# Side work of VectorE in a fused attention and expert kernel, handed out by the room of each step

## The chip, the cores and the metric

The kernel runs on one core of one Trainium2 chip. The metric is device time in microseconds (us) of one execution; three runs of the kernel before are shown. Engines are named as in the profile: PE is TensorE's matmul and PEld its weight load, DVE is VectorE, ACT is ScalarE, POOL is GpSimd, SP is SyncE, which here only issues transfers.

## The reference

The input is a tensor of 2 batches, 256 channels and 56 x 56 places (3136 tokens per batch). Layer 0 is a non-local block without a softmax, with normalisation, residual and relu. Layer 1 is causal attention with 4 heads of 64, and then a mixture of 8 experts of which each token takes 2. Cut to what matters here:

```python
t = _to_tokens(x)                                   # 2 x 3136 x 256
t = t + _L1_attn_ref(_ln_t(t), W_attn, W_proj)      # q, k, v; softmax(q k / 8, causal) v; W_proj
t = t + _L1_ffn_ref(_ln_t(t), gate_w, gate_b, W1, b1, W2, b2)
# ffn: probs = softmax(xf @ gate_w); the two best experts per token;
#      out += prob[e] * (gelu(xf @ W1[e] + b1[e]) @ W2[e] + b2[e])
```

## The kernel before, in words

All data is f32. Layer 0 comes first and ends at about 90 us. Then come the attention of both batches (about 90 to 845 us), and the experts (845 us to the end). Within the attention, the order of every engine's instructions is the order in which the Python code issues them; nothing reorders it.

**Steps.** Queries are cut into 7 blocks of 448 columns (`W`, index `i`), heads into 2 pairs (`hp`), and keys into chunks of 128 (`j`). One step is one chunk of keys against one block of queries for one pair of heads. A step has two halves: `scores(n)` (matmuls on L804, the exponential on ScalarE on L808, for a chunk on the diagonal a mask on VectorE on L811, and VectorE's running sum of the exponentials on L822 or L827), and `values(n)` (matmuls on L855). The values run `LAG` = 3 steps behind the scores. Masked chunks, called cut, and whole chunks alternate at the end of each block; a cut chunk has fewer columns to do. In the last step of a block and pair, ScalarE copies the values out of their bank (L862), and GpSimd adds the two halves into `qT` (L863). The pool of the values' bank (`py`) has one buffer, that of the scores (`psc`) two, that of the exponentials (`st`) five.

**Visits.** Two steps behind the end of each block and pair (`BEHIND`, with the lag), the loop makes a visit: `visit` issues the matmuls of the projections ahead (queries and keys L613, values L628, transposes L599), and `products` those of the output projection (L682), with one add each on VectorE (L687). Behind it `sum_rows` sums the exponentials over the keys with matmuls of ones (L876), copies the result on ScalarE (L881) and stores it with four transfers on SP, and reads it back with a fifth.

**Later.** A list `later`, kept by a step counter `clock`, holds what follows on the sums: `invert` (a reciprocal of 7 columns on VectorE, L896, and three transfers) 4 steps on, `scale` (VectorE multiplies `qT` by the inverses, L908) 6 steps on, and `hand_on` 2 steps on, which allows the output projection of that block.

**Side work.** Generators in a queue hold the rest: statistics of finished rows (`closer`, L177 and L178, two instructions per chunk of 128 tokens), the choice of experts (`choose`, `dispatch`: some hundred small VectorE instructions per batch), scatters of the rows to their experts' slots (L1493 on VectorE, L1501 on GpSimd, two scatters per chunk), and loads of the experts' first weights on SP. One call of `pull` issues one piece. `between` is called once per step, ahead of its scores, and pulls one piece in every step, except in cut steps of block 0:

```python
tick[0] += 1
if not cut or i:
    pull()
```

In the last block of the last batch `between` also issues loads of the experts' second weights (`load_w2`). In the experts' stage `meanwhile` pulls what is left.

Of the kernel before, what the change touches and what calls it, by code (L numbers as in the profile page):

```python
# [28 lines left out]
def conv_attn_moe_kernel(  # L29
# [52 lines left out]
    P = 128  # L82
    B, C, N = x.shape
    NH = C // P
# [8 lines left out]
    W = 448  # L93
    NB = N // W
# [54 lines left out]
    def room(name):  # L149

        return tok.tile([P, NH * E * H], F32, tag="room", name=name)
# [18 lines left out]
    sum_d = nc.dram_tensor("sums", (NSUM, 2, W), F32, kind="Internal").ap()  # L170
# [340 lines left out]
    def layer1(nm, general):  # L511

        with ExitStack() as whole:
# [182 lines left out]
                    yield False  # L696

            unclosed = [NCH] * B

            def closer(b, first, m, k):  # L700

                for n in range(first, first + m):
                    stats(b, n, 1, k, bg, f"o{nm}{b}")
                    unclosed[b] -= 1
                    yield True

            def attend(qT, kT, v, fst, fs, psc, py, open_batch, visit, between, clock, later, finished):
# [156 lines left out]
                        del yps[b, hp, i]  # L864

                def sum_rows(b, hp, i):
                    yh = qT[:, hp, i * W : (i + 1) * W]
                    r = (b * NH + hp) * NB + i
                    sn = f"{nm}{b}_{hp}_{i}"
                    acc = accs[b, hp, i]  # L870
                    summed.add((b, hp, i))
                    sp = bank(f"sp_{b}_{hp}_{i}")

                    flat = acc.rearrange("p a w -> p (a w)")
                    for g in range(4):
                        nc.tensor.matmul(  # L876
                            sp[g * 32 : (g + 1) * 32, : W // 2], ones[:, :32],
                            flat[:, g * W // 2 : (g + 1) * W // 2], start=True, stop=True,
                        )
                    line = fs.tile([P, W], F32, tag="rb", bufs=3, name=f"line_{sn}")  # L880
                    nc.scalar.copy(line[:, : W // 2], sp[:, : W // 2])  # L881
                    halves = sum_d[r].rearrange("a (h w) -> (a h) w", h=2)
                    for g in range(4):
                        nc.sync.dma_start(
                            out=halves[g : g + 1], in_=line[g * 32 : g * 32 + 1, : W // 2]
                        )
                    nc.sync.dma_start(
                        out=sums[:, r], in_=sum_d[r].rearrange("a (p f) -> (a p) f", p=HS)
                    )
                    later.append((clock[0] + 4, invert, b, hp, i, yh))  # L890

                def invert(b, hp, i, yh):
                    r = (b * NH + hp) * NB + i
                    sn = f"{nm}{b}_{hp}_{i}"
                    back = fs.tile([P, 2 * W // P], F32, tag="back", name=f"back_{sn}")
                    nc.vector.reciprocal(back, sums[:, r])  # L896
                    nc.sync.dma_start(
                        out=inv_d[r].rearrange("a (p f) -> (a p) f", p=HS), in_=back
                    )
                    rb = fs.tile([P, W], F32, tag="rb", bufs=3, name=f"rb_{sn}")  # L900
                    for a in range(2):
                        nc.sync.dma_start(
                            out=rb[a * HS : (a + 1) * HS], in_=inv_d[r, a].partition_broadcast(HS)
                        )
                    later.append((clock[0] + 6, partial(scale, rb), b, hp, i, yh))

                def scale(rb, b, hp, i, yh):
                    nc.vector.tensor_tensor(yh, yh, rb, ALU.mult)  # L908
                    later.append((clock[0] + 2, hand_on, b, hp, i, yh))

                def hand_on(b, hp, i, yh):
# [2 lines left out]
                def due(now):  # L914
                    while later and (now is None or later[0][0] <= now):
                        _, task, b, hp, i, yh = later.pop(0)
                        task(b, hp, i, yh)
                        later.sort(key=lambda e: e[0])

                ends = {s[:2]: n for n, s in enumerate(steps)}  # L920
                LAG, BEHIND, FREED = 3, 2, 4
                visits = {BEHIND: (0, -1, NH - 1)}
# [4 lines left out]
                final = visits.pop(len(steps) + BEHIND)  # L927
                visits[len(steps) + 1] = final
                for n in range(len(steps) + LAG):
                    if n in visits:  # L930
                        visit(*visits[n])
                        b, i, hp = visits[n]
                        if i >= 0 and visits[n] != final:
                            sum_rows(b, hp, i)
                        aligned()
                    if n + 1 < len(steps) and n > LAG and steps[n][2] == 0 and steps[n - LAG - 1][2] == 0 and steps[n - LAG - 1][4]:
                        turn_rows(*steps[n][:2])
                    if n < len(steps):
                        b, i = steps[n][:2]
                        if n == 0 or steps[n - 1][0] != b:  # L940
                            open_batch(b)
                        between(b, i, ends[b, i] - n, (steps[n][3] + 1) * P > i * W + 1)

                    late = n >= LAG and steps[n - LAG][4]
                    if n >= LAG:
                        due(clock[0])
                        clock[0] += 1
                    if n >= LAG and not late:
                        values(n - LAG)
                    if n < len(steps):  # L950
                        scores(n)
                    if late:
                        values(n - LAG)
                sum_rows(final[0], final[2], final[1])
                return due

            def attend_general(b, qT, kT, v):
# [1128 lines left out]
            else:  # L2086
# [54 lines left out]
                def visit(b, i, hp):  # L2141

                    now, then = ahead(b, i, hp)
                    last = b + 1 == B and i + 1 == NB
                    if last and hp == 0:
                        assert ranked[0]
                        early_ids.extend(experts_of(0))
                    if last and hp + 1 == NH:
                        nc.scalar.activation(warm, eps5[:1], AF.Gelu)
                        while len(early_rows) < 2:  # L2150
                            pull(every=True)
                        now = [partial(early_input, n, qT) for n in range(2)]
                    ring.append(0)
                    for piece in now:
                        piece()
                    for _ in range(2):
                        products()
                    for piece in then:
                        piece()
                    ring.clear()  # L2160

                def between(b, i, left, cut):
                    if b == B - 1 and i == NB - 1 and left < NH * NCH - 2:

                        now = load_w2(left < NCH - 4)
                        for _ in range(1 if left > NCH - 4 else 2):
                            next(now, None)

                    tick[0] += 1
                    if not cut or i:  # L2170
                        pull()

                due = attend(
# [259 lines left out]
```

## Time and profile before

| | us |
|---|---|
| median of three runs | 1254.82 |
| lowest and highest | 1254.31, 1254.89 |
| profiled execution, its own time | 1272.23 |
| span of its instructions | 1270.5 |
| PE busy | 1247.3 |
| DVE busy | 773.9 |
| ACT busy | 613.1 |
| POOL busy | 356.2 |
| running sums L827, DVE | 344.5 in 344 instructions |
| exponentials L808, ACT | 330.7 in 400 instructions |

The span runs from the first to the last instruction of the one profiled execution. The mean granted clock of TensorE in it is 0.995. Busy times are sums over the span; PE's overlap its weight loads, and its ends are modelled. A line such as L827 is a line of the kernel before.

### The profile page before, as it was taken

Reading aid. Unit: us, or ns where it says so; the run is one execution under the profiler, and the core shown is the slowest. Engines: PE = TensorE matmul, PEld = TensorE weight load, DVE = VectorE, ACT = ScalarE, POOL = GpSimd, SP = SyncE. Lnnn points to the kernel's source line nnn. Section 1 sums busy time; section 2 is a strip of 40 time slices with the busy share of each in tenths; the row PEclk is TensorE's granted clock in tenths of the full one; section 3 lists DMA queues with packets and bytes.
Section 4 is the critical chain, followed back from the end, with each engine's and each line's share of the span. In section 5 each row is a group of like instructions: output and inputs, shape, how many; then the busy total and the mean of one; then the engine's idle time right before and its main releaser. Section 6 shows DMA issues by size and latency. Waiting matters only on the chain.

```text
span 1270.5 us, 28742 instructions
## 1 busy us (share of the span) xinstructions
PE 1247.3 (98%) x10881; PEld 857.1 (67%) x10881; DVE 773.9 (61%) x1687; ACT 613.1 (48%) x1237; POOL 356.2 (28%) x318
## 2 busy tenths in 40 slices
PE   8999999999999999999999999999999999999998
PEld 8876655555454645655555543469888999899996
DVE  2683567566766575576677887785743433455664
ACT  0255555565656565455555655563332333344442
POOL 1103231110021104211112766100266112666651
PEclk9999999999999999999999999999999999999999
DMA  9995101000000000100000223641344343466654
GB/s 314 354 345 187 25 23 37 25 15 26 14 17 16 7 20 17 36 21 14 9 16 25 71 67 110 202 136 61 101 135 151 101 114 101 142 200 200 212 164 125
DMA packets 118723, 125.66 MB, mean 99 GB/s; under 512 B 27223, under 2 KB 108488, under 8 KB 118578
## 3 DMA queue, kind: packets, MB, share of 16 engines
q1 hardware_dynamic: 107922, 97.19, 25.3%
q0 software_dynamic: 9840, 25.67, 6.0%
q8 instruction: 90, 1.47, 0.5%
q10 hardware_dynamic: 816, 0.88, 0.2%
q14 instruction: 55, 0.45, 0.1%
HBM read 62.06 MB, written 61.05 MB: 97 GB/s over the span
## 4 chain that ended last, share of the span: by engine, by line
PE 91%; DVE 4%; DMA 1%; issue 1%; ACT 1%; SPq 0%; DVEq 0%; ACTq 0%
PE sc_f L804 19%; PE yp_f L855 18%; PE ht_f L1637 14%; PE yp_f L1656 14%; PE qk_f L613 7%; PE v_f L628 4%; PE pp_f L682 3%; PE cp L410 3%; PE gram L317 2%; DVE acc_f L827 2%; PE tp_f L1614 2%; PE sp_f L876 1%; PE xp_f L599 1%; PE yo_f L1883 1%; DMA w1s_f<-in_w_dram 0%
## 5 line engine op out<-in xcount | busy, mean ns | idle before, releaser
L808 ACT ACTIVATE st_f<-sc_f 128x896 f32<-128x896 f32 (+5 forms) x400 | 330.7, 838 | 198.0 <-PE sc_f L804 178.9
L827 DVE TENSOR_TENSOR acc_f<-acc_f,st_f 128x896 f32<-128x896 f32 (+6 forms) x344 | 344.5, 1002 | 118.9 <-ACT st_f L808 109.1
L804 PE MATMUL sc_f<-qT_f,kT_f 64*64 64x448 f32 (+5 forms) x3136 | 347.5, 499 | 0.3 <-ACT st_f L808 0.3
L855 PE MATMUL yp_f<-st_f,v_f 64*64 64x448 f32 (+5 forms) x2928 | 328.0, 510 | 4.1 <-ACT acc_f L862 2.5
L804 PEld LDWEIGHTS sc_f<-qT_f,kT_f 64*64 64x64 f32 x3136 | 144.8, 133 | 128.9 <-issue 106.2
L1646 ACT ACTIVATE g_f<-ht_f,b1b 128x128 f32<-128x128 f32 x408 | 116.6, 371 | 227.3 <-PE ht_f L1637 123.4
L855 PEld LDWEIGHTS yp_f<-st_f,v_f 64*64 64x64 f32 x2928 | 125.1, 133 | 132.2 <-issue 99.3
L1637 PE MATMUL ht_f<-xT_f,w_f 128*128 128x128 f32 x1600 | 196.9, 276 | 5.2 <-issue 5.2
L1637 PEld LDWEIGHTS ht_f<-xT_f,w_f 128*128 128x128 f32 x1600 | 193.8, 192 | 9.1 <-issue 4.6
L1501 POOL DMA_INDIRECT x_slots<-xr_f,idx x100 | 120.4, 1204 | 147.0 <-DVE xr_f L1499 77.6
L863 POOL TENSOR_TENSOR qT_f<-acc_f 128x448 f32<-128x448 f32 x26 | 29.6, 1140 | 406.3 <-ACT acc_f L862 406.3
L1625 DVE COPY w_f<-w1s_f 128x1024 f32 x102 | 72.7, 713 | 90.0 <-PE ht_f L1637 34.2
L584 POOL TENSOR_SCALAR xn_f<-t 128x256 f32<-128x256 f32 (+1 forms) x50 | 82.4, 1655 | 129.4 <-DVE t L185 43.6
L1677 POOL DMA_INDIRECT y_tokens<-ys_f,to_f x57 | 59.2, 1038 | 125.2 <-DVE ys_f L1666 102.9
L613 PE MATMUL qk_f<-px_f,wat 128*128 128x512 f32 (+2 forms) x224 | 88.2, 546 | 0.6 <-ACT px_f L605 0.6
L1666 DVE TENSOR_TENSOR ys_f<-yp_f,kT_f 128x128 f32<-128x128 f32 x102 | 29.5, 289 | 92.3 <-PE yp_f L1656 69.5
L613 PEld LDWEIGHTS qk_f<-px_f,wat 128*128 128x128 f32 x224 | 40.6, 190 | 46.3 <-issue 41.7
L1656 PE MATMUL yp_f<-px_f,g_f 128*128 x204 | 62.3, 387 | 1.6 <-issue 1.6
L1656 PE MATMUL yp_f<-kT_f,g_f 128*128 x204 | 62.1, 386 | 0.0
L1656 PE MATMUL yp_f<-v_f,g_f 128*128 x204 | 61.8, 385 | 0.0
L1656 PE MATMUL yp_f<-w2s_f,g_f 128*128 x204 | 61.6, 384 | 0.0
L1834 POOL DMA_INDIRECT y_f<-y_slots,idx x50 | 55.5, 1110 | 17.1 <-issue 17.1
(299 smaller groups left out, 1302.4 us busy)
## 6 DMA issues: line engine op xcount, KB each, us to landing
x_slots<-fill SPq DMA_DIRECT2D x1, 8190.0 KB
xb_f<-x_slots SPq DMA_DIRECT2D x60, 130.0 KB
x_slots<-fill SPq DMA_DIRECT2D x1, 7296.0 KB
y_slots<-ys_f SPq DMA_DIRECT2D x57, 128.0 KB
kept<-t SPq DMA_DIRECT2D x2, 3200.0 KB
x<-in_x_dram SPq DMA_DIRECT2D x14, 448.0 KB
rb_f<-inverses SPq DMA_DIRECT2D x56, 112.0 KB
y_f<-y_tokens SPq DMA_DIRECT2D x23, 256.0 KB
```

The costliest lines, as they stand in the source:

```text
L584: nc.gpsimd.tensor_scalar(xn[:k, a], ts[b][:k, n + a, :C], ts[b][:k, n + a, MEAN : MEAN + 1], ts[b][:k, n + a, RSTD : RSTD + 1], ALU.subtr ...
L613: nc.tensor.matmul(ps[:, :w], wat[:, c, d0 : d0 + P], px[:, s % 2, c, :w], start=(c == 0), stop=(c == NH - 1),)
L804: nc.tensor.matmul(to, left, right, start=True, stop=True)
L808: nc.scalar.activation(st[rows, :, c0:], ps[rows, :, c0:W], AF.Exp, scale=SCALE)
L827: nc.vector.tensor_tensor(acc[rows, :, c0:], acc[rows, :, c0:], st[rows, :, c0:], ALU.add)
L855: nc.tensor.matmul(to, left, right, start=first, stop=end)
L1501: s = nc.gpsimd.indirect_dma_start(out=xds[b], out_offset=bass.IndirectOffsetOnAxis(ap=idxs[b][:kk, k, n : n + 1], axis=0), in_=xr[:kk], i ...
L1625: nc.vector.tensor_copy(w, w1s[:, :, bass.ds(e, 1), :].rearrange("p c e h -> p c (e h)"))
L1637: nc.tensor.matmul(ht[:, k, :], w[:, c, k * P : (k + 1) * P], xT[:, c, :], start=(c == 0), stop=(c == NH - 1),)
L1646: nc.scalar.activation(g[:, k, :], ht[:, k, :], AF.Gelu, bias=b1bs[b][:, k, i : i + 1])
L1656: nc.tensor.matmul(yp[:, :C], g[:, k, :], w2s[k][:, bass.ds(e, 1), :].rearrange("p e d -> p (e d)"), start=(k == 0), stop=(k == KH - 1),)
L1677: s = nc.gpsimd.indirect_dma_start(out=y_tokens, out_offset=bass.IndirectOffsetOnAxis(ap=to[:, n % GB : n % GB + 1], axis=0), in_=ys, in_o ...
```

## The change

It does four things.

1. A balance `spare`, in us, decides on side work. `room(n)` gives what a step leaves to VectorE: 1.5 us for a full block of columns, less 0.42 for a mask, less 0.07 + 1.02 for the running sum, scaled by the width. `between` adds it (to a balance of at most 1.0) and pulls a piece when the balance is above -0.8 (-0.9 while scatters of the first batch go on), which costs 0.35 (0.3). Statistics take another 0.25, a scaling 0.6.
2. A visit adds 2.0 to the balance (at most 2.0 in all), and at its end pulls pieces at 0.5 each (0.8 while sending) until the balance is 0.3 or less.
3. `sum_rows` issues the matmuls alone and returns the rest, `store_sums`, which is called behind the values of that step (when those are not a block's first). As the clock has been advanced by then, what follows on the sums is due one step later than before.
4. The scaling of the last block of the last batch is due 9 steps behind its inverses, the others 6.

The number of instructions on each compute engine and the work in them are the same.

```diff
             unclosed = [NCH] * B
+            spare = [0.0]
...
                 for n in range(first, first + m):
                     stats(b, n, 1, k, bg, f"o{nm}{b}")
+                    spare[0] -= 0.25
                     unclosed[b] -= 1
                     yield True
...
                 def sum_rows(b, hp, i):
...
                             flat[:, g * W // 2 : (g + 1) * W // 2], start=True, stop=True,
                         )
+                    return partial(store_sums, b, hp, i, sp)
+
+                def store_sums(b, hp, i, sp):
+                    yh = qT[:, hp, i * W : (i + 1) * W]
+                    r = (b * NH + hp) * NB + i
+                    sn = f"{nm}{b}_{hp}_{i}"
                     line = fs.tile([P, W], F32, tag="rb", bufs=3, name=f"line_{sn}")
                     nc.scalar.copy(line[:, : W // 2], sp[:, : W // 2])
...
-                    later.append((clock[0] + 6, partial(scale, rb), b, hp, i, yh))
+                    loading = b == B - 1 and i == NB - 1
+                    later.append((clock[0] + (9 if loading else 6), partial(scale, rb), b, hp, i, yh))

                 def scale(rb, b, hp, i, yh):
                     nc.vector.tensor_tensor(yh, yh, rb, ALU.mult)
+                    spare[0] -= 0.6
                     later.append((clock[0] + 2, hand_on, b, hp, i, yh))
...
+                def room(n):
+
+                    _, i, _, j, first, _, _ = steps[n]
+                    off = j * P - i * W
+                    width = W - max(0, off)
+                    return (
+                        2 * 0.75 * width / W
+                        - (0.42 if off > -P else 0)
+                        - (0 if first else 0.07 + 1.02 * width / W)
+                    )
...
                 for n in range(len(steps) + LAG):
+                    copy_sums = None
                     if n in visits:
                         visit(*visits[n])
                         b, i, hp = visits[n]
                         if i >= 0 and visits[n] != final:
-                            sum_rows(b, hp, i)
+                            copy_sums = sum_rows(b, hp, i)
                         aligned()
...
-                        between(b, i, ends[b, i] - n, (steps[n][3] + 1) * P > i * W + 1)
+                        between(b, i, ends[b, i] - n, (steps[n][3] + 1) * P > i * W + 1, room(n))

                     late = n >= LAG and steps[n - LAG][4]
                     if n >= LAG:
                         due(clock[0])
                         clock[0] += 1
                     if n >= LAG and not late:
                         values(n - LAG)
+                    if copy_sums:
+                        copy_sums()
                     if n < len(steps):
                         scores(n)
                     if late:
                         values(n - LAG)
-                sum_rows(final[0], final[2], final[1])
+                sum_rows(final[0], final[2], final[1])()
                 return due
...
                 def visit(b, i, hp):
...
                     for piece in then:
                         piece()
                     ring.clear()
-
-                def between(b, i, left, cut):
+                    spare[0] = min(spare[0] + 2.0, 2.0)
+                    while spare[0] > 0.3:
+                        spare[0] -= 0.8 if placed[0] and not sent[0] else 0.5
+                        pull()
+
+                def between(b, i, left, cut, room):
...
                     tick[0] += 1
-                    if not cut or i:
+                    spare[0] = min(spare[0], 1.0) + room
+                    sending = placed[0] and not sent[0]
+                    if spare[0] > (-0.9 if sending else -0.8):
+                        spare[0] -= 0.3 if sending else 0.35
                         pull()
```

More of the change, by code (lines that the diff above doesn't have):

```diff
@@ L866, in sum_rows @@
                 def sum_rows(b, hp, i):
-                    yh = qT[:, hp, i * W : (i + 1) * W]
-                    r = (b * NH + hp) * NB + i
-                    sn = f"{nm}{b}_{hp}_{i}"
                     acc = accs[b, hp, i]
@@ L879, in sum_rows @@
                         )
+                    return partial(store_sums, b, hp, i, sp)
[3 more added lines that the diff above has]
+                    sn = f"{nm}{b}_{hp}_{i}"
                     line = fs.tile([P, W], F32, tag="rb", bufs=3, name=f"line_{sn}")
                     nc.scalar.copy(line[:, : W // 2], sp[:, : W // 2])
-                    halves = sum_d[r].rearrange("a (h w) -> (a h) w", h=2)
+                    split = sum_d[r].rearrange("a (h w) -> (a h) w", h=2)
                     for g in range(4):
                         nc.sync.dma_start(
-                            out=halves[g : g + 1], in_=line[g * 32 : g * 32 + 1, : W // 2]
+                            out=split[g : g + 1], in_=line[g * 32 : g * 32 + 1, : W // 2]
                         )
```

## The prediction

> **What bounds the kernel now.** I read the page's busy shares and chain first, then the waits of TensorE, then the timeline at each of those waits. The busy line and the chain say that TensorE sets the time almost everywhere:
>
> ```profile
> PE 1247.3 (98%) x10881; PEld 857.1 (67%) x10881; DVE 773.9 (61%) x1687; ACT 613.1 (48%) x1237; POOL 356.2 (28%) x318
> ...
> PE 91%; DVE 4%; DMA 1%; issue 1%; ACT 1%; SPq 0%; DVEq 0%; ACTq 0%
> ```
>
> The first line is busy us per engine, the second the shares of the chain that ended last. So work taken from VectorE or ScalarE is worth nothing as such; only moments count in which TensorE waits for them. The waits of TensorE list these (us in total, times, longest):
>
> ```profile
> PE yp_f L855 <- ACT acc_f L862: 2.5, 4, 0.7
> PE yp_f L855 <- DVE st_f L811: 1.4, 3, 0.8
> ```
>
> The second row is what the change aims at: values held by VectorE's mask (L811). The longest stands in the timeline, in the second batch, four steps behind a projection:
>
> ```profile
> 519.28 1.32 DVE L827 TENSOR_TENSOR acc_f<-acc_f,st_f 128x896 f32<-128x896 f32 x1 [2.16 <-ACT st_f L808]
> ...
> 520.52 0.41 DVE L177 BATCH_NORM_STATS2 st_of<-t 128x6 f32<-128x256 f32 x1
> ...
> 523.38 1.24 PE L804 MATMUL sc_f<-qT_f,kT_f 64*64 64x448 f32 x8
> 523.90 0.42 DVE L177 BATCH_NORM_STATS2 st_of<-t 128x6 f32<-128x256 f32 x1
> 524.35 0.18 DVE L178 BATCH_NORM_AGGREGATE t<-st_of 128x2 f32<-128x6 f32 x1
> 524.45 0.61 DVE L908 TENSOR_TENSOR qT_f<-qT_f,rb_f 128x448 f32<-128x448 f32 x1
> ...
> 524.97 0.42 DVE L811 TENSOR_TENSOR st_f<-st_f,keep 128x256 f32<-128x256 f32 x1
> 525.42 0.69 DVE L827 TENSOR_TENSOR acc_f<-acc_f,st_f 128x512 f32<-128x512 f32 x1
> 525.45 0.66 PE L855 MATMUL yp_f<-st_f,v_f 64*64 64x192 f32 x8 [0.82 <-DVE st_f L811]
> ```
>
> Columns: start, us, engine. See that VectorE stood idle 2.16 us just before 519.28, and that the same engine then had three statistics pairs and a scaling handed to it within the narrow masked steps, so the mask came late. Scores start at 523.38 and the values behind them at 525.45: 2.07 us, where a full step in steady state takes 0.75 from scores to values (303.15 to 303.90 in the timeline). The loss is 1.32 us, more than the 0.82 shown as idle, as the pipe had to drain.
>
> **What the Trainium skill says.** "Perfetto Trace Analysis", Per-instruction lifecycle: a matmul's end is modelled, so starts are safer than ends; that is why I measure from start to start, and the 1.32 against 0.82 agrees. "TensorE: Matmul & The Clock Gate", Architectural detail: ScalarE and VectorE take their queues strictly in order. The lines above agree: the ready mask waits behind a scaling nobody is waiting for. "VectorE: DVE Perf Modes", Specifications and Mode 1x: 0.96 GHz, one f32 result a cycle for two tensors, so 896 take 0.93 us by estimate; the trace has 1.09, which I use. "GPSIMD Engine Reference", Specifications: GpSimd shares VectorE's SBUF ports when an instruction has two SBUF inputs; the add at 519.28 took 1.32 beside two GpSimd normalisations, against 1.09 alone, so crowding side work into projections is not free.
>
> **The change part by part.** No instruction is added or removed; the order moves.
>
> *Side work by room.* A full, unmasked step leaves 1.5 - 1.09 = 0.41 us by the new function's own constants, and a pull costs 0.35, so full steps go on pulling; masked steps leave nothing or less and skip. A visit (the place of the projections) gives 2.0 of credit, so up to four pulls follow it, three when sending or when statistics charge their 0.25. In the changed order, statistics that stood one per step on three or four steps behind a projection stand together behind the projection's adds. Worked out at the stall above: 2 pairs of 0.42 + 0.18 and one scaling of 0.61 move into the 2.16 us idle, 1.81 in all, so it fits; what is left in the four steps is the later scaling, one step further on, and the last pair, two further on. I take 1.3 us back. In the first batch the same place (scores 150.30, values 151.29) lost 0.99 - 0.75 = 0.24. The other masked steps where TensorE took longer than for the same step in the other batch or head pair, start of scores to start of scores: 166.46 (1.08 against 0.81), 169.04 (0.66 against 0.52), 654.64 (1.02 against 0.52), 723.72 (0.73 against 0.60), 758.56 (0.88 against 0.60). With the 0.24 these are 1.5; statistics or a scaling stand ahead of the mask in each, and the new order shifts most by one step to a full one. I take 1.0. The rank products, now inside a visit, leave step 624.95 but need a bank there: 0.
>
> *Scaling one step later.* The clock is read after it is advanced, so invert, scale and hand-on run a step later in all blocks. In blocks 1 to 4 this moves the scaling (0.61) from a masked to a full step (counted above), in block 5 from a full to a masked one, four times: unseen before, bounded by 0 and 4 x 0.3; I take +0.2 in all, as VectorE shows 0.4 us idle per full step there.
>
> *Sums' copy behind the values.* ScalarE's copy of the sums (0.345) now stands behind its copy of the values (0.91) and ahead of the exponential:
>
> ```profile
> 517.12 0.34 ACT L881 COPY line_f<-sp_f 128x224 f32<-128x224 f32 x1
> ...
> 517.52 0.91 ACT L862 COPY acc_f<-yp_f 128x896 f32<-128x896 f32 x1
> ...
> 518.32 1.63 ACT L808 ACTIVATE st_f<-sc_f 128x896 f32<-128x896 f32 x2
> ```
>
> There the sums' copy ended at 517.46, before the values were done, so the values' copy gains nothing; at the waits for L862 of 476.35 it likewise ended first. Gain 0, at most 4 x 0.35 = 1.4. The exponential behind is 0.35 later, 27 times. Its values are needed three steps on: at 520.78 for an exponential that ended at 519.24, 1.5 us to spare; in the narrow block 0, the mask ended at 477.80 and the values started at 478.30, 0.5 to spare. So 0 (upper bound 27 x 0.35 = 9.3). Behind it on ScalarE wait only exponentials; the five SP transfers of the sums go about 1 us later, covered by invert's extra step. On GpSimd scatters go ahead of one or two additions of 1.14, whose reader, the scaling, is a step later too.
>
> *The last block's scaling.* VectorE waited there for a transfer:
>
> ```profile
> 826.00 0.62 DVE L908 TENSOR_TENSOR qT_f<-qT_f,rb_f 128x448 f32<-128x448 f32 x1 [1.66 <-DMA rb_f<-inverses]
> ```
>
> It then ran without a gap until the values at 840.03 waited 0.22 for a mask. Three steps (4.5 us) more cover 1.66 with the weights' loads, now pulled a few steps earlier, in front of it on SP. I take 0.3. "DMA: Bandwidth & Descriptors" gives about 2.0 us fixed per transfer; here the inverses took 4.2 amid the loads, so the slack is used.
>
> **The sum:** -1.3 - 1.0 + 0.2 + 0 - 0.3 = -2.4; statistics gone from full steps also let VectorE enter the masked steps less late, in some 20 further blocks where the loss is under 0.1 each and I saw none singly: 0 to -1.5, I take -0.6. That makes -3.0. The profiled execution took 1272.2 (span 1270.5 and 1.7 around it), so 1269.2; it stands 17.4 above the median of 1254.8. The stalls counted lie before 845 us, where the granted clock reads 1.00, so I carry them one for one: 1254.8 - 3.0 = **1251.8**. A measurement of this kernel can tell about 0.2%, 2.5 us, from no change.
>
> **Rivals.** *Slower: the exponential's 0.35 us.* Place: the first step behind each of 27 sums. If later exponentials never catch up before TensorE asks, all are bare: +9.3 - 3.0, 1261.1. It decides once about 16 of 27 are bare (5.5 us). For it: ScalarE's copies in a visit already queue. Against: ScalarE idles 0.5 to 0.6 us before each full exponential (row after row of the timeline), so 0.35 is made good in one step. *No change:* the stall at 525 is replaced by another, ScalarE or the values' single bank being next, or the bunched statistics overrun the 2.16 us (a fourth pair would make 2.4) and delay the following masks: half the gain, 1253.6. For it: the sums of small savings are guesses. *Larger gain:* the values' copy does come earlier at the four waits of 2.5 us and these, drained pipe included (0.4 each), vanish: 2.5 + 1.6, 1254.8 - 3.0 - 4.1 = 1247.7. Against: the ends given above. *Not what it says:* room is an estimate; if side work just piles up before masks, it is the no-change case.
>
> **How the numbers follow.** Main case 0.55 (own range 1249.5 to 1253.5, about 0.85 of it beyond -2.5), larger gain 0.13, no change 0.19, slower 0.13. Faster: 0.47 + 0.13 = 0.60; same: 0.08 + 0.19 = 0.27; slower: 0.13. The range takes the main case, half of the larger gain and the upper edge of no change, and a third of the slower: 1247.5 to 1257.0.
>
> **What would show it.** Right: the row of values waiting for L811 falls from 1.4 us to under 0.5; behind that projection three statistics pairs in one run and no wait at the fourth step; the last block's scaling without a DMA wait; the row for L862 near 2.5. Wrong: exponentials that TensorE waits for, a larger L811 row, or new waits on statistics, ScalarE's copies or banks in visits; a gain above 5 us would say that L862's row or losses outside the attention were the larger part.

## The result, and the profile after

The changed kernel took 1252.82 us (median of 22 runs, 1252.02 to 1253.94), the kernel before, run beside it, 1254.82 (22 runs, 1253.89 to 1255.86): a ratio of 0.9985, 95% interval 0.9979 to 0.9990. That is 2.0 us less, by the interval 1.3 to 2.6; a gain, but inside the 0.2% that the prediction called no change. A second series gave nearly the same ratio, 0.9986 (below).

The profiled execution took 1252.24 us (span 1250.5). Its span can't be set against the span before of 1270.5: that trace has stretches at half clock and idle times of TensorE put down to "issue" in the experts' stage, and this one has neither there. I therefore compare the attention stage alone, from the start of the first step's scores to the start of the last step's, step by step. It took 739.19, 738.86 and 738.32 us in three traces of the kernel before, and 735.53 and 735.54 us in two of the changed one: 2.8 us less against the best of the former.

The busy line and the chain of the page after:

```profile
PE 1238.0 (99%) x10881; PEld 852.2 (68%) x10881; DVE 775.4 (62%) x1687; ACT 613.3 (49%) x1237; POOL 348.7 (28%) x318
...
PE 48%; DVE 1%; issue 0%; ACT 0%; DVEq 0%
```

The counts of instructions are those of before: only the order has moved. The shares of the chain add up to 49%, as the page could follow it back to 631 us and no further; in that part it runs almost wholly through TensorE. For the part ahead of it the waits of TensorE have to do. TensorE's waits (total us, times, longest):

```profile
PE yp_f L857 <- ACT acc_f L864: 1.7, 3, 0.6
...
PE yp_f L857 <- DVE st_f L813: 0.3, 1, 0.3
PE total_f L1283 <- ACT px_f L605: 0.2, 1, 0.2
```

(Line numbers have moved: values L857, their copy L864, mask L813, adds L829, scaling L914, sums' copy L886.) The wait for the mask fell from three to one of 0.3 us; the wait for the copy of the values lost one of its four times. The place of the longest stall, behind the second batch's projection, in VectorE's timeline after:

```profile
515.75 0.42 DVE L177 BATCH_NORM_STATS2 st_of<-t 128x6 f32<-128x256 f32 x1
516.20 0.18 DVE L178 BATCH_NORM_AGGREGATE t<-st_of 128x2 f32<-128x6 f32 x1
516.30 0.39 DVE L177 BATCH_NORM_STATS2 st_of<-t 128x6 f32<-128x256 f32 x1
516.73 0.18 DVE L178 BATCH_NORM_AGGREGATE t<-st_of 128x2 f32<-128x6 f32 x1
516.83 0.40 DVE L177 BATCH_NORM_STATS2 st_of<-t 128x6 f32<-128x256 f32 x1
517.26 0.18 DVE L178 BATCH_NORM_AGGREGATE t<-st_of 128x2 f32<-128x6 f32 x1
517.36 0.60 DVE L914 TENSOR_TENSOR qT_f<-qT_f,rb_f 128x448 f32<-128x448 f32 x1
518.79 1.11 DVE L829 TENSOR_TENSOR acc_f<-acc_f,st_f 128x896 f32<-128x896 f32 x1 [0.83 <-ACT st_f L810]
...
522.68 0.41 DVE L813 TENSOR_TENSOR st_f<-st_f,keep 128x256 f32<-128x256 f32 x1
523.13 0.69 DVE L829 TENSOR_TENSOR acc_f<-acc_f,st_f 128x512 f32<-128x512 f32 x1
523.74 0.62 DVE L914 TENSOR_TENSOR qT_f<-qT_f,rb_f 128x448 f32<-128x448 f32 x1
```

Three statistics pairs and a scaling stand in one run inside what was idle time; 0.83 of 2.16 us idle is left. The next scaling stands behind the mask of 522.68 instead of ahead of one: each of the two runs a step later than before, and for the first the next step lies behind the projection. TensorE at that step:

```profile
522.65 1.24 PE L806 MATMUL sc_f<-qT_f,kT_f 64*64 64x448 f32 x8
523.40 0.70 PE L857 MATMUL yp_f<-st_f,v_f 64*64 64x192 f32 x6
```

Scores to values is 0.75 us, the steady distance, where it was 2.07.

All steps whose time differs by 0.1 us or more between the best trace of before and the trace after (start of scores to start of scores; a step is named by its time in the first trace before):

| step, us | before | after | difference |
|---|---|---|---|
| 150.30 and the next | 1.36 + 7.65 | 1.08 + 7.93 | 0.00 |
| 166.46 | 1.07 | 0.82 | -0.25 |
| 171.2 and the two next, 546.4 and the two next | 11.29 each | 11.29 each | 0.00 |
| 503.0 and the next | 1.19 + 12.90 | 1.38 + 12.72 | 0.00 |
| 523.38 and the next | 2.44 + 8.86 | 1.08 + 9.16 | -1.06 |
| 624.95 and 628.39 (rank products moved) | 2.57 + 6.25 | 1.53 + 7.44 | +0.15 |
| 654.64 | 1.02 | 0.83 | -0.19 |
| 682.8 and 685.5 (a product of the experts' biases moved) | 1.50 + 2.76 | 2.71 + 1.50 | -0.04 |
| 688.3 | 0.73 | 0.84 | +0.11 |
| 723.72, 758.56 | 0.70, 0.88 | 0.60, 0.60 | -0.38 |
| 766.95 | 3.06 | 2.25 | -0.81 |
| 798.33 | 0.80 | 0.52 | -0.28 |

These make -2.75; all smaller differences together -0.04. The steps of 171.2 and 546.4 are each 0.10 shorter by themselves, but the two steps behind them are 0.10 longer together.

### The profile page after: what moved, and what is told of

Same layout as the page of the kernel before. It is cut to its first block, busy times and chain, and to the rows that moved or that the text cites. A ratio compares the mean times of both kernels' runs of the same rounds, so it can differ in the third digit from the quotient of the medians.

```text
span 1250.5 us, 28749 instructions
## 1 busy us (share of the span) xinstructions
PE 1238.0 (99%) x10881; PEld 852.2 (68%) x10881; DVE 775.4 (62%) x1687; ACT 613.3 (49%) x1237; POOL 348.7 (28%) x318
## 5 line engine op out<-in xcount | busy, mean ns | idle before, releaser
L829 DVE TENSOR_TENSOR acc_f<-acc_f,st_f 128x896 f32<-128x896 f32 (+6 forms) x344 | 344.0, 1000 | 108.9 <-ACT st_f L810 99.9
L857 PE MATMUL yp_f<-st_f,v_f 64*64 64x448 f32 (+5 forms) x2928 | 327.6, 510 | 2.0 <-ACT acc_f L864 1.7
L857 PEld LDWEIGHTS yp_f<-st_f,v_f 64*64 64x64 f32 x2928 | 126.2, 133 | 129.0 <-issue 102.4
L1522 POOL DMA_INDIRECT x_slots<-xr_f,idx x100 | 112.3, 1123 | 140.8 <-DVE xr_f L1520 71.2
```

The costliest lines, as they stand in the source:

```text
L829: nc.vector.tensor_tensor(acc[rows, :, c0:], acc[rows, :, c0:], st[rows, :, c0:], ALU.add)
L857: nc.tensor.matmul(to, left, right, start=first, stop=end)
L1522: s = nc.gpsimd.indirect_dma_start(out=xds[b], out_offset=bass.IndirectOffsetOnAxis(ap=idxs[b][:kk, k, n : n + 1], axis=0), in_=xr[:kk], i ...
```

## The experiments

Three series ran, each on one chip. On the chips of the first and the third the kernel before takes 1266.7 and 1266.8 us, on that of the second 1254.72. Times are compared within a series only. Up to about 700 us the steps of the attention repeat to 0.02 us (one step of one trace: 0.06) from trace to trace and chip to chip where the order is the same, so there a single trace tells parts apart that the times can't; later, on the slower chips, single steps are longer by 0.2 to 0.7 us, in other places in each kernel. Steps go on being named by their time in the first trace of the kernel before.

**The kernel before again**, unedited, first series:

> The kernel before, unchanged, run against itself. It tells two things: how far apart two equal kernels come out (I expect a ratio of 1.000 with an interval of about 0.0005), and which of the losses in the first profile of before recur. Theory: the loss of 1.3 us behind the second batch's third block (scores at 523.38) recurs, as the order of instructions makes it; the two delays at 766.95 and 783.68 (0.95 and 0.52 us) do not, as nothing in the order accounts for them. Rival: they recur too, and then 1.5 us of the gain in the profile belong to the change.

Measured: 1266.78 us, ratio 1.0003 (0.9992 to 1.0014); the interval is 0.11% either way, where I had expected 0.05%. Attention stage 738.86 us. The extra 0.52 us at 783.68 of the first trace is not there: chance. The long step of 766.95 is there again, with 3.08 us: not chance, as I had taken it to be.

**Side work by room alone.** The sums' copy stays in its old place, the last block's scaling at six steps:

```diff
-                            copy_sums = sum_rows(b, hp, i)
+                            sum_rows(b, hp, i)()
...
-                    later.append((clock[0] + (9 if loading else 6), partial(scale, rb), b, hp, i, yh))
+                    later.append((clock[0] + 6, partial(scale, rb), b, hp, i, yh))
```

> The changed kernel with the side work by room alone: the sums' copy stands ahead of the values again, what follows on the sums is due as before, and the last block's scaling is due after 6 steps. Theory (the gain comes from VectorE's side work): 1253.0 to 1253.6, the larger part of the 2.0 us; the wait of the values for the mask at the third block is gone or small. Rival (the gain comes from the sums' copy or from the step by which the chain of the sums is later): 1254.6 or more, and the wait stays.

Measured: 1268.62 us, ratio 1.0011 (1.0001 to 1.0020): no gain in time, against the expectation, though its attention stage of 737.68 us is 1.2 shorter than that of the kernel before on this chip. The trace shows in part why the stage gained no more. The step of 523.38 fell only from 2.44 to 1.90, the one of 766.95 from 3.08 to 2.25, and new stalls came, at 688 (0.73 to 1.15), 690 (0.60 to 1.19) and 712 (1.50 to 2.14). The first of them in the timeline of this kernel:

```profile
686.54 0.41 DVE L1514 TENSOR_SCALAR xr_f<-t 128x256 f32<-128x256 f32 x1
...
686.87 0.62 DVE L914 TENSOR_TENSOR qT_f<-qT_f,rb_f 128x448 f32<-128x448 f32 x1
...
687.40 0.42 DVE L813 TENSOR_TENSOR st_f<-st_f,keep_f 128x256 f32<-128x256 f32 x1
...
687.88 0.76 PE L857 MATMUL yp_f<-st_f,turn_f 64*64 64x320 f32 x8
```

A row scaling that the room granted and the attention's scaling stand back to back ahead of the mask; the values start as the mask ends. The scaling is not handed out by room: it has a due step, and in this kernel that step is a masked one. What took the 1.2 us back outside the attention is not shown: in the traces from this chip the experts' stage alone lies between 419.2 and 421.0 us.

**The sums' copy behind the values alone.** The kernel before with that move, which also makes the chain behind it one step later:

```diff
-                            sum_rows(b, hp, i)
+                            copy_sums = sum_rows(b, hp, i)
...
+                    if copy_sums:
+                        copy_sums()
```

> The kernel before with the sums' copy behind the values alone (and with it the chain of the sums one step later); side work one piece per step as before, 6 steps to the scaling. Theory: within 0.7 us of before, 1254.2 to 1255.2, since the copy that it moves is not what the values' copy waits for; what it does save comes by the later scaling in the third block (at most 0.7). Rival (the values' bank comes free earlier): 1253 or less, and TensorE's waits for the values' copy fall from 2.5 us to under 1. Rival (exponentials 0.35 us later): 1256 or more.

Measured: 1267.00 us, ratio 1.0001 (0.9992 to 1.0010). The step of 523.38 took 1.92, the one of 166.46 0.82 instead of 1.08; 766.95 kept its length (3.05). Attention stage 738.39 us.

**Only the later chain.** The kernel before, with the inversion due one step later and the copy where it was:

```diff
-                    later.append((clock[0] + 4, invert, b, hp, i, yh))
+                    later.append((clock[0] + 5, invert, b, hp, i, yh))
```

> The kernel before with the inverses of the sums due 5 steps behind the sums instead of 4, so that the scaling comes one step later, and nothing else. Theory: the scaling leaves the masked step of the third block, so the wait there falls from 0.82 us of idle time by about 0.4 to 0.6, and the time by 0.3 to 0.8 us: 1254.0 to 1254.5. Rival (statistics alone make the wait): no change, 1254.8. Equal to the run with the sums' copy alone if the copy itself is worth nothing.

Measured: 1267.06 us, ratio 0.9999 (0.9991 to 1.0008). Its steps before 700 us are those of the moved copy to within 0.04 us (523.38: 1.89, 166.46: 0.82). At 723.72 both were longer than before, 1.20 and 1.12 against 0.70 us, and at 758.56 this one, 1.35 against 0.88: alone, the later chain also costs. Attention stage 738.76 us, 0.1 less than before on this chip; the times can't show the 0.3 to 0.8 us that I had forecast.

**Room and the later chain, without the moved copy.** Side work by room alone, with the inversion at +5:

```diff
-                    later.append((clock[0] + 4, invert, b, hp, i, yh))
+                    later.append((clock[0] + 5, invert, b, hp, i, yh))
```

> Side work by room, the sums' copy left in its old place behind the sums' product, and the inversion told one step later by its due time (clock + 5 instead of + 4), so that the scaling falls where it falls in the changed kernel. Without the later inversion this kernel had an attention stage of 737.68 us, with stalls of 0.42, 0.58 and 0.63 us at the steps of 688, 690 and 712 us that the changed kernel does not have. Theory A: what the moved copy brings is the later scaling, not ScalarE's order; then the attention stage is 735.5 to 735.9 us, those three stalls are gone, and the step four behind the second batch's projection takes 1.1 us instead of 1.9. Theory B: ScalarE's order itself matters (the values' copy 0.35 us earlier); then the stage stays at 737.2 to 737.7 us. In the times against the kernel before: A gives about -1.7 us, B about 0.

Measured: 1266.54 us, ratio 1.0001 (0.9991 to 1.0010); attention stage 737.41 us, so the total expected under A was not met. The places named were: the step of 523.38 takes 1.08, those of 688, 690 and 712 take 0.84, 0.51 and 1.50, all as in the changed kernel; of the other steps before 720 us none differs from it by over 0.05 us apart from two (0.10 us shorter at 544, 0.13 longer at 717). The excess of 1.9 us lies mostly in later steps (around 724: +0.40, 746: +0.53, 782: +0.27, 796: +0.43); another kernel of this series, the changed one with four copies split (the second such kernel below), is 0.66 longer at the same step of 746. So A holds where traces repeat: the copy's move acts through the later step. What lengthens the late steps on this chip stays open. The same doubt touches the 0.63 us at 712 with room alone, not the pair at 688 and 690, whose cause its timeline shows.

**The changed kernel again**, second series:

> The changed kernel once more, beside the others of this series on one chip, as the mark for their differences. Theory (the change saves time on TensorE's queue in the attention stage alone): ratio to the kernel before about 0.9985, near 2 us less, and an attention stage about 735.5 us long in the trace, 3.3 to 3.7 us shorter than before's 738.9 to 739.2. Rival (the 2.0 us were a matter of where the two kernels ran): ratio 1.000 within 0.1%, or an attention stage that is not 735 to 736 us.

Measured: 1253.09 us against 1254.72, ratio 0.9986 (0.9978 to 0.9993); attention stage 735.54 us. The first theory holds.

**The last block's scaling at six steps**:

```diff
-                    later.append((clock[0] + (9 if loading else 6), partial(scale, rb), b, hp, i, yh))
+                    later.append((clock[0] + 6, partial(scale, rb), b, hp, i, yh))
```

> The changed kernel with the last block's scaling at six steps as before; the side work by room and the sums' copy behind the values stay. My theory, from the prediction's own sum: the three steps are worth 0.3 us, so this is 0.0 to 0.5 us longer than the changed kernel, and its attention stage 735.5 to 736.0 us. The wait of VectorE's scaling for its DMA (1.66 us in the kernel before, at 826) comes back without TensorE waiting for it. Rival (the last block is where the change earns its gain: the scaling would hold VectorE's queue ahead of the masked steps): 1 us or more longer, with a new stall of TensorE near 826.

Measured: 1252.70 us, ratio 0.9984 (0.9977 to 0.9990); attention stage 735.61 us, 0.07 from the changed kernel. By the traces the three steps are worth 0.07 us, less than the 0.1 by which such late steps differ between them; by the times nothing. The wait for the transfer did not come back either; VectorE's timeline of this kernel and then of the changed one:

```profile
822.59 0.62 DVE L914 TENSOR_TENSOR qT_f<-qT_f,rb_f 128x448 f32<-128x448 f32 x1
```

```profile
826.05 0.62 DVE L914 TENSOR_TENSOR qT_f<-qT_f,rb_f 128x448 f32<-128x448 f32 x1
```

Neither has the bracket with the 1.66 us of before. Three traces of the kernel before show this wait with 1.66, 2.22 and 1.09 us; with the side work by room alone, and with the later inversion alone, it is gone, and with the sums' copy moved alone 0.5 is left.

**Four sums' copies**, to price late exponentials:

```diff
-                    nc.scalar.copy(line[:, : W // 2], sp[:, : W // 2])
+                    for _ in range(4):
+                        nc.scalar.copy(line[:, : W // 2], sp[:, : W // 2])
```

> The changed kernel with the sums' copy of each block made four times in a row on ScalarE, the same copy to the same place. It prices the slower case of the prediction: how late the exponentials may come. Each of 27 blocks then has three copies of 0.35 us more, 1.05 us, ahead of what ScalarE does next. If the exponentials' lateness reaches TensorE whole (the slower rival): 27 x 1.05 = 28 us longer. If a wide step's 0.5 us of room on ScalarE covers part of it once: 27 x 0.5 = 14 us longer. My theory, that ScalarE's room of one or two steps and the scores made ahead cover it: 0 to 4 us longer, with TensorE's waits for the exponentials (scores waiting for the bank, values waiting for the exponential) at a few block ends only.

Measured: 1268.89 us, ratio 1.0106 (1.0091 to 1.0122), 15.8 us over the changed kernel; attention stage 15.1 us longer. My theory was wrong by far; the middle reading comes nearest. In this kernel's timeline a group of copies takes 1.49 us, 1.14 more than one:

```profile
263.07 0.91 ACT L864 COPY acc_f<-yp_f 128x896 f32<-128x896 f32 x1 [1.00 <-issue]
263.88 1.49 ACT L887 COPY line_f<-sp_f 128x224 f32<-128x224 f32 x4
265.26 0.92 ACT L810 ACTIVATE st_f<-sc_f 128x896 f32<-128x896 f32 x1
```

and TensorE's waits have a new row on top:

```profile
PE sc_f L806 <- ACT st_f L810: 7.1, 26, 0.4
```

Behind wide blocks the step became 0.44 us longer and the next one 0.05, nearly every time alike; behind narrow ones it was 0.48 to 0.65 and again 0.05. So about 0.65 us of 1.14 is covered behind a wide block, 0.45 to 0.6 behind a narrow one. The rest is lost to TensorE at once; the steps behind make good 0.15 of it at most, in some narrow blocks.

**Without the pulls in a visit**:

```diff
-                    spare[0] = min(spare[0] + 2.0, 2.0)
-                    while spare[0] > 0.3:
-                        spare[0] -= 0.8 if placed[0] and not sent[0] else 0.5
-                        pull()
```

> The changed kernel without the credit and the pulls in a visit (the place of the projections); between steps the side work still goes by room. Theory: the pulls in the visit put statistics and a scaling into VectorE's idle time behind a projection, and that is what empties the step four behind it; without them side work is only skipped, so the same work comes later or into fewer steps: the stall at the second batch's block 2 stays at 0.5 to 1.4 us (in the changed kernel 0), and the attention stage is 736.5 to 738.5 us against 735.5. Rival: skipping narrow steps is enough and the visit's pulls only move two small products of TensorE: 735.4 to 735.8 us.

Measured: 1297.06 us against 1266.82, ratio 1.0247 (1.0233 to 1.0261): 30 us slower, which neither theory had. The step of 523.38 itself takes 1.08 here, too: with the later chain, skipping the narrow steps was enough for that stall, as the rival said. Its attention stage is 739.46 us all the same, longer than either theory allowed, with three waits for exponentials (1.2 us) late in it. But the side work was then not done in time. TensorE's waits begin with

```profile
PE first_f L1556 <- DMA xb_f_first<-x_slots: 20.6, 1, 20.6
```

and the scatters that this load needs (GpSimd, L1522) run over the end of the attention:

```profile
846.59 0.93 POOL L1522 DMA_INDIRECT x_slots<-xr_f,idx  x1 [0.31 <-issue]
847.82 0.92 POOL L1522 DMA_INDIRECT x_slots<-xr_f,idx  x1 [0.30 <-issue]
853.96 1.86 SPq L2045 DMA_DIRECT2D xb_f_first<-x_slots  x4
```

In the changed kernel the fifty scatters of the attention stage are over by 840 us; here six of them come after it. The first expert's load, which SP holds until the last of them has landed (853.84 by the trace's events), then goes out at 853.96 and the transpose starts at 860.88. From the last scores on this trace has 447.8 us, 27 more than the kernel of room and later chain on the same chip (420.9), 20.6 of it this wait. So the visit's pulls keep the side work's pace.

**The values' copy in halves**, at the four first blocks, where TensorE's three waits for it lie: one half on ScalarE, one on VectorE.

```diff
-                        nc.scalar.copy(both, yp[:, :, :W])
+                        if i:
+                            nc.scalar.copy(both, yp[:, :, :W])
+                        else:
+                            nc.scalar.copy(both[:, 0], yp[:, 0, :W])
+                            nc.vector.tensor_copy(both[:, 1], yp[:, 1, :W])
```

> A candidate: the changed kernel with the copy of the values of each head pair's first block (four of 28) made in two halves, one on ScalarE, one on VectorE, which stands idle there. In the changed kernel TensorE waits 0.57, 0.59 and 0.57 us for that copy of 0.91 us (at 118, 475 and 488). Theory: each half takes about 0.5 us, so each of the three waits falls to 0.1 or 0.2 us: 1.2 us less than the changed kernel, and the row of values waiting for the copy falls from 1.7 to below 0.6 us. Rival (another wait takes its place: the exponentials behind the copy): the row falls but the attention stage gets shorter by under 0.5 us.

Measured: 1254.34 us, ratio 0.9998 (0.9990 to 1.0006), attention stage 736.53 us: 1.0 us worse. VectorE's half (0.62 us) started only when ScalarE's (0.53 us) had ended, 1.19 together for 0.91.

**The same with a tile of its own for VectorE's half**:

```diff
+                            part = fs.tile([P, W], F32, tag="rb", bufs=3, name=f"part_{sn}")
...
-                            nc.vector.tensor_copy(both[:, 1], yp[:, 1, :W])
+                            nc.vector.tensor_copy(part, yp[:, 1, :W])
...
+                            nc.gpsimd.tensor_tensor(yh, both[:, 0], part, ALU.add)
```

> The candidate with the split copy of the values, mended: VectorE's half goes to a tile of its own, since with one tile VectorE's half (0.62 us) started only when ScalarE's (0.53 us) had ended, and the values behind it came 0.3 us later than in the changed kernel at four places. Theory: with a tile of its own the halves run side by side, the waits of 0.57, 0.59 and 0.57 us shrink by 0.91 - 0.62 = 0.29 us each where VectorE is free: attention stage 734.6 to 735.0 us. Rival: both halves read the same bank and still go one after the other: 736.3 to 736.6 us as with one tile.

Measured: 1267.16 us, ratio 1.0002 (0.9993 to 1.0010). ScalarE's half and VectorE's in the timeline:

```profile
118.21 0.53 ACT L869 COPY acc_f<-yp_f 128x448 f32<-128x448 f32 x1
```

```profile
118.78 0.62 DVE L870 COPY part_f<-yp_f 128x448 f32<-128x448 f32 x1 [6.58 <-ACT acc_f L869]
```

118.21 + 0.53 = 118.74: one after the other again, although the targets are apart. The four places are 0.25 to 0.29 us longer, as before. So the rival's order holds, but not its total: the attention stage is 738.03 us, and most of the 1.5 us over the rival's range lies in late steps (746: +0.66, 758.56: +0.26, 780: +0.23). The bracket says what puts the halves in a row: VectorE's half waits for ScalarE's semaphore, in all four places of both kernels, and starts 0.03 us after ScalarE's half. The wait thus stands in the built program, and whether the chip could do both halves at once was not tried.

**The kernel before, once more with a trace**, third series:

> The kernel before, profiled on the chip of the other runs of this call, for its experts' stage. The changed kernel's attention stage is 3.3 us shorter by the traces, its time only 1.6 to 2.0 us less. Theory A: the experts' stage is the same in both (409.2 us from the last scores to the end, as in every trace of the changed kernel), and the rest of the difference is scatter of the first stage, which took 99.9 to 102.2 us in the traces so far. Theory B: the kernel before has a shorter experts' stage by 1.3 us, 407.9 us: part of the gain is given back there.

Measured: 1266.51 us, ratio 0.9999 (0.9987 to 1.0010); attention stage 738.32, experts' stage 421.4 us. This chip too has the long experts' stage (420 to 421 us for all kernels that ran here, but for the late scatters above; 409.2 in all five traces of the second series' chip and of the first result). Neither theory is settled: no trace of the kernel before comes from a chip with the short stage.

## Why the prediction came out as it did

The time forecast, 1251.8, lies 1.0 us under what was measured; the sum of -3.0 is near the trace's -2.8 in the attention stage. That it came so near is in part luck: 1.09 of the 2.8 come from two steps for which the sum has no term.

- **The stall behind the second batch's projection, -1.3.** The step itself gave 1.36, but the next gave 0.30 back: -1.06. The two causes named, the statistics out of the narrow steps and the scaling a step later, each give half alone: 0.54 with room, 0.52 with the copy's move, 0.55 with the later inversion, 1.06 with both. So one cause alone would have been worth 0.5, not 1.3. That the statistics ran in the idle time behind the projection was right as a picture but not needed for this stall: without the visit's pulls, but with the later chain, the step is as short.
- **The other masked steps, -1.0.** The five named apart from 150.30 gave -0.25, -0.04, -0.19, -0.10 and -0.28 (against the best trace of before), together -0.86, for 0.76 in the sum. At 150.30 the 0.28 came back at once in the next step. I had measured what a step loses, not whether its neighbour was shorter for it.
- **Scaling in block 5, +0.2; rank products, 0.** No step there is longer; the rank products cost 0.15 in their visit.
- **Sums' copy, 0 in ScalarE's order.** Right: room with the later inversion and the copy in its old place repeats the changed kernel's steps. The exponentials' 0.35 us is covered: no step behind a sum is longer than before, nor is there a new wait for exponentials; but the reason given, that a lateness is made good in one step and 1.5 us are to spare, was too generous. The four copies show 0.45 to 0.65 us of cover.
- **The last block's scaling, -0.3.** Wrong: 0.0. The wait for the transfer was VectorE's and hardly reached TensorE, and room alone or the later inversion alone removes it without the three steps.
- **Some 20 further blocks, -0.6.** Wrong: no such small gains are left over (the smaller differences make -0.04, and the 0.10 at 171.2 and at 546.4 went back in the steps behind). What stood in their place was two single steps: 766.95 (-0.81) and 798.33 (-0.28). Both are long in every kernel without room (3.05 to 3.20 and 0.79 to 0.93), short with room (2.25 and 0.51 to 0.59; the four copies make 0.45 more at the first), and long again without the visit's pulls (2.85 and 0.81). What failed is the reading of the trace before: the sum has no term for the 3.2 us of 766.95, which I took for chance even after the result, as no mask stands there. It was the fourth wait of the values for their copy, whose row I had forecast to stay "near 2.5" and which fell to 1.7. In the kernel before, the copy there began 1.64 us after ScalarE's last work, released by the trace only as scores of the next step ended:

```profile
765.12 0.98 PE L855 MATMUL yp_f<-st_f,v_f 64*64 64x448 f32 x8
...
765.93 1.68 PE L804 MATMUL sc_f<-qT_f,kT_f 64*64 64x448 f32 x16
...
767.25 0.91 ACT L862 COPY acc_f<-yp_f 128x896 f32<-128x896 f32 x1 [1.64 <-PE sc_f L804]
...
768.21 0.61 PE L855 MATMUL yp_f<-st_f,v_f 64*64 64x448 f32 x4 [0.60 <-ACT acc_f L862]
```

The values end at 766.10 by the trace; with room alone the copy began within 0.15 us of their end (values from 765.97 for 0.98 us, copy at 767.06). The events of the trace name what held it: TensorE's own semaphore. Behind the sums (765.24) it rises next at 767.18, 0.07 us ahead of the copy; with room alone it rises at 766.99, 0.04 behind the modelled end of the values. So in the kernel before the values were done, or were told of, 1.1 us late on TensorE itself. All six traces without room or without the visit's pulls have this (0.9 to 1.3 us late); in all the others the copy starts 0.11 us behind the values. Why TensorE was late is not settled, nor what made 798.33 long.

- **The price of crowding.** The prediction puts the 1.32 us of the add at 519.28, against 1.09 alone, down to two GpSimd normalisations. GpSimd's addition of the values' halves lies over the start of that add, too:

```profile
518.51 1.14 POOL L863 TENSOR_TENSOR qT_f<-acc_f 128x448 f32<-128x448 f32 x1 [14.30 <-ACT acc_f L862]
...
519.63 3.91 POOL L584 TENSOR_SCALAR xn_f<-t 128x256 f32<-128x256 f32 x2
```

Five adds of this size that meet the end of such an addition in the same way (0.37 us) and no normalisation took 1.32 as well; adds beside normalisations alone took 1.06 to 1.28. In the changed kernel most of these adds meet 0.12 us of the addition and take 1.09, and three that lie over the whole of it take 2.33 to 2.45. No wait of TensorE for such an add stands in the profiles.

- **From the trace to the time.** The trace's -2.8 became -2.0 (1.3 to 2.6) and -1.6 (0.9 to 2.8) in the two timed comparisons. That the stages outside the attention give up to 1 us back was not shown nor ruled out. On the slower chips the changed kernel itself was not timed; the nearest to it, room and later chain, shows no gain there (1.0001).

Of the rivals, the slower one names a true mechanism. It had each block either bare or covered; the runs show a cover of 0.45 to 0.65 us per block, under which 0.35 costs nothing and above which every block pays. ("No change" as half the gain would be 1253.3 by the sum of 3.0, not 1253.6; the measured time is under both.) "No change" foresaw that other waits would follow on the first, which the trace shows with room alone, at 688 and 690. "Larger gain" asked for all four waits for the copy to vanish; one did.

## What to carry to other kernels

When side work is moved away from narrow steps, name where it runs instead and by when it must be done: without the visit's pulls the same stall was gone, but the kernel took 30 us more, 20.6 of them because the last scatters held the next stage's load. Work with a fixed due step and work handed out by room share one queue, so an estimate of room that doesn't see the due work can put both ahead of the same mask. Sum a stall over the step and its neighbours before booking it, and look at each wait of the critical engine, those that seem chance too, in a second trace.

## What the runs showed of the hardware

- The same kernel took 1254.8 us where the first result was taken and 1254.7 in the second series, but 1266.7 and 1266.8 on the chips of the first and third; in the traces the difference lies in the experts' stage (409 against 419 to 421 us), where TensorE is idle for 6 to 8 us instead of 0.3, 4 to 6 of them for no reason that the profile shows. An effect of 0.15% must be timed on one chip.
- Up to about 700 us one trace repeats another to 0.02 us per step (once 0.06) where the order is the same. There a step table separates edits of 0.3 us that the timed runs, with intervals of about 0.1% (1.3 us) either way, do not.
- Half of the values' copy, 128x448, took 0.53 us on ScalarE and 0.62 us on VectorE, the whole 0.91 on ScalarE: from these, by estimate, 0.15 us of a copy on ScalarE does not depend on size.
- In the 20.6 us in which TensorE waited (no visit's pulls), its granted clock stood at 0.50 (850 to 861 us), and at 0.74 on the mean of the five us behind; the changed kernel shows 1.00 over 840 to 870 us.
- VectorE's add of 128x896 took 1.09 us alone, 1.32 where it met the last 0.37 us of GpSimd's addition, and 2.33 to 2.45 where it lay over the whole of that.
